# A relational graph layer on one core: the gate's u turned by DMA in two-byte halves instead of by TensorE

## The chip, the cores and the metric

The kernel runs on one core of a Trainium2 chip. The metric is the device time of one execution in microseconds (us). A core has TensorE (PE; its weight loads are listed as PEld), VectorE (DVE), ScalarE (ACT), GpSimd (POOL) and SyncE (SP), each with a queue of its own that it works off in order, and 16 DMA engines that move data for the queues of SP, ACT and POOL. Engines wait for one another by semaphores.

## The reference

With h = relu(layernorm(x)) for 1250 nodes of 1024 values, and 20000 edges of 8 types:

```python
def _rgcn(x, edge_index, edge_type, weight, root, bias):
    ...
    out = x @ root + bias
    for r in range(weight.shape[0]):
        ...
        mean = sums / jnp.maximum(cnt, 1.0)[:, None]
        out = out + mean @ weight[r]
    return out
u = _rgcn(x, edge_index, edge_type, weight, root, bias)
z = jnp.concatenate([u, x], axis=1) @ w_gate + b_gate
h = jnp.tanh(u) * z + x * (1.0 - z)
```

`x` stands here for the layer's input h; what is returned is the first x plus this result. All arrays are float32. The part that matters below is the gate's product u @ w_gate[:1024], which needs u with its columns on the partitions, that is, transposed.

## The kernel before

The nodes lie in 10 blocks of 128 rows (the last has 98), taken in 5 pairs. Each of the matrices (8 weights, root, the two halves of w_gate) is multiplied with a pair of blocks by one call of `product`, which forms seven products of half-size blocks in place of eight. `transposed` puts a block, turned, into the operand tile `h_op` at A11 and A12 (first block of a pair) or A21 and A22 (second block): eight transposes on TensorE into two PSUM banks, then one copy on ScalarE (L378) and one on VectorE (L376). `left` then makes four sums of these on VectorE (L387): S1 = A21 + A22, S2 = S1 - A11, S4 = A12 - S2, S3 = A11 - A21. The seven products of a pair read A11, S1, S2, S4, S3, A12 and A22, in this order (in the last pair A11, A12, S1, S2, S3, S4, A22).

Between the products the results are put together. ScalarE copies the bank after A11 (L457), after S1 (L469), after S2 (L489) and after S3 (L430); VectorE adds after S4 (L423), S3 (L431) and A12 (L448). The products of A11, S2, S3 and A22 go one after the other onto the same bank, those of S1 and S4 onto another, so a product that adds onto a bank starts only after the copy of what stood there.

After each product `product` calls `between(j)`, j from 0 to 6. In the gate, the last of the stages, that is `beside_u` (`beside_last` for pair 5), which issues the work for later pairs. The queues are written out by hand: every engine works in the order in which the program issues. In the gate loop, with i from 0 to 4 for pairs 1 to 5, it is:

- j = 0: gathers of the rows of x + h for pair i (`xhs`), gathers that add z's rows onto the bias that lies in z's place (for pair 1 at j = 3), loads of u for pair i + 2 (L1691, SP) and gathers of its rows of h @ root;
- j = 1: scatters of the finished rows of the pair before (L746);
- j = 2: the bias loads for pair i + 1 (L1649, SP); z * d and + xhs (L1667, L1668, for pair 1 at j = 5); u of pair i + 2 gets its rows of h @ root added (L1611); gathers of h rows for pair i + 1 and its tanh (L1676);
- j = 3: transposes and `left` for pair i + 1;
- j = 4: d = tanh(u) - h for pair i + 1 (L1684);
- j = 3 to 5 and after the last product: `finish` (L1733, L1734), row = product * d + z.

All gathers go by L740 on GpSimd's queue. Those of xhs, of h @ root and of h land in tiles from `got()`, a pool of five buffers of 128 x 1024 float32, given out in program order: a new tile waits until one of the five has been read for the last time. u has a pool of four such buffers.

Of the kernel before, what the change touches and what calls it, by code (L numbers as in the profile page):

```python
# [9 lines left out]
F32 = mybir.dt.float32  # L10
BF16 = mybir.dt.bfloat16
I32 = mybir.dt.int32
AF = mybir.ActivationFunctionType
OP = mybir.AluOpType
AX = mybir.AxisListType
# [4 lines left out]
def tile_rgcn_highway(  # L20
# [31 lines left out]
    nc = tc.nc  # L52
# [3 lines left out]
    P = 128  # L56
# [8 lines left out]
    NP = ND // 2  # L65
# [18 lines left out]
    A11, A12, A22, S1, S2, S3, S4 = range(7)  # L84
    A21 = S3
# [100 lines left out]
    class Second:  # L186
# [22 lines left out]
        def left(self):  # L209
            nc.vector.tensor_add(self.s1, self.a21, self.a22)  # L210
            nc.vector.tensor_sub(self.s2, self.s1, self.a11)
# [152 lines left out]
    def transposed(aop, part, of, n, relu=False):  # L364


        for half, to in enumerate(((A11, A12), (A21, A22))[part]):
            p = bank().rearrange("p (k f) -> p k f", k=KQ)
            for i in range(KQ):
                k = KQ * half + i  # L370
                nc.tensor.transpose(p[:, i, :n], of[:n, k * P:(k + 1) * P], ident[:n, :n])  # L371
            to_n, p_n = aop[:, to, :, :n], p[:, :, :n]
            if half and relu:
                nc.vector.tensor_scalar_max(to_n, p_n, 0.0)
            elif half:
                nc.vector.tensor_copy(to_n, p_n)  # L376
            else:
                nc.scalar.activation(to_n, p_n, AF.Relu if relu else AF.Copy)  # L378
            if n < P:
                nc.gpsimd.memset(aop[:, to, :, n:], 0.0)  # L380

# [354 lines left out]
    h_op = [keep.tile([P, 7, KQ, P], F32, name=f"h_op{i}") for i in range(NP)]  # L736
# [73 lines left out]
    with ExitStack() as early:  # L810
# [483 lines left out]
        while going[0]:  # L1294
            s, i = next(steps)
# [11 lines left out]
    with ExitStack() as edges_part:  # L1307
# [7 lines left out]
        def got():  # L1315
            t = gpool.tile([P, D], F32, name="got")
            if fresh[0]:
                nc.gpsimd.memset(t, 0.0)
                fresh[0] -= 1
            return t  # L1320
# [25 lines left out]
        us = {}  # L1346
# [202 lines left out]
        while s < R0[1]:  # L1549
            step(s, i, on)  # L1550
            s, i = next(steps)
# [14 lines left out]
        s, i = beside(first_group, sum(K[0]) + LATE + 1, s, i, R0[2] - 1)  # L1566
# [46 lines left out]
        def place_of(what, i, part):  # L1613

            o = ("z", "d").index(what)
            if i % 2:
                w = fac[NM - 1].spare[o].rearrange("p k n -> p (k n)")
                return w[:, part * D:(part + 1) * D]
            return h_op[2 + o][:, 2 * part:2 * part + 2].rearrange("p a k f -> p (a k f)")

        def pair(i):
            return [(part, 2 * i + part, nrows(2 * i + part)) for part in range(2)]
# [46 lines left out]

        def gate_u(i, j):  # L1670

            if j == 2:
                for part, d, n in pair(i):
                    hs[part] = got()
                    rows_of(hs[part][:n], h_dram[:, :], node[:n, LG, d:d + 1])
                    nc.scalar.activation(place_of("d", i, part)[:n], us[d][:n], AF.Tanh)  # L1676
            elif j == 3:
                for part, d, n in pair(i):
                    transposed(h_op[i % 2], part, us.pop(d), n)
                left(h_op[i % 2])  # L1680
            elif j == 4:
                for part, d, n in pair(i):
                    dt = place_of("d", i, part)
                    nc.vector.tensor_sub(dt[:n], dt[:n], hs[part][:n])  # L1684

        def gate_load(i, j):

            if j == 0:
                for part, d, n in pair(i):
                    u = new_u(d)  # L1690
                    nc.sync.dma_start(u[:n], last_dram[d * P:d * P + n, :])  # L1691
                    adds.append(add_hr(d, u))
            elif j == 2:
                while adds:
                    adds.pop(0)()
# [28 lines left out]
        for i in range(NP):  # L1724
            t = [rows.tile([P, D], F32, name="row") for _ in range(2)]

            def finish(part, of, c0, more=None):
                d = 2 * i + part
                n = nrows(d)
                at = slice(c0, c0 + of.shape[-1])  # L1730
                to = t[part][:n, at]
                if more is None:
                    nc.vector.tensor_mul(to, of[:n], place_of("d", i, part)[:n, at])  # L1733
                    nc.vector.tensor_add(to, to, place_of("z", i, part)[:n, at])  # L1734
                else:
                    nc.vector.tensor_mul(more[:n], of[:n], place_of("d", i, part)[:n, at])
                    nc.vector.tensor_add(to, to, more[:n])

            def beside_u(j):
                if i == 0 and j == 0:  # L1740
                    fac[NM - 1].make_t4()
                gate_rows(i, j)
                if j == 1:
                    scatter_outs()
                if i + 2 < NP:
                    gate_load(i + 2, j)
                if j == (3 if i else 5):
                    finish(0, t[0][:, Q:], Q)
                if j == (4 if i else 5):
                    finish(1, t[1][:, Q:], Q)  # L1750
                if j == 5:
                    finish(0, t[0][:, :Q], 0)
                    outs.append((2 * i, t[0]))
                if i + 1 < NP:
                    gate_u(i + 1, j)

            def beside_last(j):
                gate_rows(i, j)
                if j == 1:
                    scatter_outs()  # L1760
                elif j == 3:
                    finish(0, t[0][:, :Q], 0)
                    finish(0, t[0][:, Q:], Q)
                elif j == 4:
                    finish(1, t[1][:, Q:], Q)
                    scatter_piece(Q, t[1])
                elif j == 5:
                    outs.append((2 * i, t[0]))
                    scatter_outs()

            def finish_last(of, c0, more=None):
# [37 lines left out]
```

## Time and profile before

| | us |
|---|---|
| median of 20 runs | 1388.38 |
| lowest, highest | 1380.16, 1399.45 |
| profiled execution | 1384.65 |
| its span | 1382.9 |
| TensorE busy | 1338.9 (97%) |
| VectorE busy | 956.0 (69%) |
| GpSimd busy | 572.7 (41%) |
| ScalarE busy | 372.5 (27%) |

The span goes from the first to the last instruction of the profiled execution; 1.75 us lie around it. The gate takes it from 1246.8 on. In the page and the answers of the trace a group is named by line, engine, operation and "out<-in" tiles; the idle time of an engine before it follows in brackets, with what ended it. A matmul of 128 x 512 float32 shows as two instructions, so the four of one product are eight.

### The profile page before, as it was taken

The page shows a single profiled execution, that of the slowest core. Times are in us where ns is not written, and L with a number is a line of the kernel's source. Part 1 is how long each engine was busy: PE and PEld are TensorE (multiplying, and loading weights), DVE is VectorE, ACT ScalarE, POOL GpSimd, SP SyncE. Part 2 cuts the span into 40 slices and gives each one's busy share as a digit, 9 for nine tenths or more (in the row PEclk, how much of TensorE's full clock was granted, in tenths as well). Part 3 has the DMA queues.
Part 4 walks back from the last instruction along what each step waited for, and adds up shares of the span by engine and source line. Part 5 has one row for each costly group of instructions (what it writes and reads, how often), then busy time and mean ns, then how long its engine had stood idle before and what let it go on. Part 6 is the DMA issues. An engine that isn't in the chain of part 4 may idle for free.

```text
span 1382.9 us, 13410 instructions
## 1 busy us (share of the span) xinstructions
PE 1338.9 (97%) x4168; PEld 728.9 (53%) x4168; DVE 956.0 (69%) x1823; ACT 372.5 (27%) x794; POOL 572.7 (41%) x509
## 2 busy tenths in 40 slices
PE   9999979996989999999999999999999999999997
PEld 5444445454535554665565565556556556544443
DVE  7744644573457446745888798788688789867975
ACT  3334535553554121221111112121112111221210
POOL 0000452555155604740345345554545556615631
PEclk9999999998999999999999999999999999999999
DMA  8745334854274424113555777977968976888971
GB/s 320 274 176 166 103 92 101 186 117 97 77 192 98 92 92 106 47 64 139 179 195 201 277 239 277 347 264 247 330 214 290 322 289 199 281 307 249 341 191 57
DMA packets 104319, 270.94 MB, mean 196 GB/s; under 512 B 20100, under 2 KB 22354, under 8 KB 104112
## 3 DMA queue, kind: packets, MB, share of 16 engines
q1 hardware_dynamic: 44048, 119.85, 27.4%
q0 software_dynamic: 44064, 118.20, 26.7%
q10 hardware_dynamic: 16128, 31.98, 7.6%
q8 instruction: 33, 0.54, 0.2%
q14 instruction: 46, 0.38, 0.1%
HBM read 212.63 MB, written 75.49 MB: 208 GB/s over the span
## 4 chain that ended last, share of the span: by engine, by line
PE 84%; issue 4%; DVE 2%; another core or an unknown queue 2%; ACT 1%; POOL 1%; DMA 0%; POOLq 0%; DVEq 0%; ACTq 0%
PE ps_b L406 41%; PE ps L406 15%; PE ps L219 14%; PE ps_n L406 4%; PE ps_b L219 4%; PE ps_q L219 2%; PE ps_q L406 2%; PE ps_n L219 1%; DMA h_op<-in_L_gnn_b_gate_dram 0%; POOL out_dram L746 0%; PE ps L371 0%; DVE junk L1145 0%; ACT is_lo L1055 0%; PE ps_q L1124 0%
## 5 line engine op out<-in xcount | busy, mean ns | idle before, releaser
L406 PE MATMUL ps_b<-w,h_op 128*128 128x512 f32 x1464 | 665.4, 599 | 6.8 <-issue 5.8
L406 PEld LDWEIGHTS ps_b<-w,h_op 128*128 128x128 f32 x1464 | 276.2, 192 | 318.5 <-issue 308.6
L1339 POOL DMA_INDIRECT got<-y,idx x193 | 249.7, 1294 | 287.5 <-DVE u L1344 182.4
L1344 DVE SCALAR_TENSOR_TENSOR u<-got,w_of,u 128x1024 f32<-128x1024 f32 (+1 forms) x193 | 246.9, 1282 | 33.9 <-DMA got<-y,idx 31.5
L406 PE MATMUL ps<-w,h_op 128*128 128x512 f32 (+1 forms) x592 | 266.3, 591 | 0.1
L1163 POOL DMA_INDIRECT table<-row_col,at_i x157 | 167.3, 1066 | 230.2 <-DVE at_i L1159 140.4
L406 PEld LDWEIGHTS ps<-w,h_op 128*128 128x128 f32 x592 | 111.3, 190 | 119.6 <-issue 115.9
L219 PE MATMUL ps<-w,w 128*128 128x256 f32 x288 | 75.3, 396 | 14.3 <-ACT w L225 12.8
L430 ACT COPY row<-ps_b 128x512 f32<-128x512 f32 x53 | 31.1, 586 | 206.5 <-PE ps_b L406 181.8
L431 DVE TENSOR_TENSOR row<-row 128x512 f32<-128x512 f32 x44 | 30.3, 690 | 78.4 <-ACT row L430 78.2
L406 PE MATMUL ps_n<-w,h_op 128*128 128x512 f32 x176 | 80.1, 592 | 0.0
L489 ACT COPY row<-ps_b 128x512 f32<-128x512 f32 x54 | 31.7, 586 | 169.9 <-PE ps_b L406 158.9
L219 PEld LDWEIGHTS ps<-w,w 128*128 128x128 f32 x288 | 56.4, 198 | 38.3 <-issue 15.2
L219 PE MATMUL ps<-w,h_op 128*128 128x256 f32 x288 | 74.5, 381 | 0.0
L1132 DVE TENSOR_TENSOR own<-ps_q,is_at 128x160 f32<-128x160 f32 (+1 forms) x40 | 12.7, 318 | 83.6 <-PE ps_q L1069 31.2
L219 PE MATMUL ps<-inner,inner 128*128 128x256 f32 x264 | 68.6, 383 | 0.0
L219 PEld LDWEIGHTS ps<-w,h_op 128*128 128x128 f32 x288 | 54.0, 190 | 27.1 <-issue 21.9
L529 ACT COPY row<-ps_b 128x512 f32<-128x512 f32 x40 | 23.4, 585 | 162.9 <-PE ps_b L406 130.7
L219 PEld LDWEIGHTS ps<-inner,inner 128*128 128x128 f32 x264 | 50.8, 192 | 14.8 <-issue 8.4
L1145 DVE SCALAR_TENSOR_TENSOR junk<-k_bc,key_col,before 128x128 f32<-128x128 int32 x157 | 55.0, 350 | 4.2
L406 PEld LDWEIGHTS ps_n<-w,h_op 128*128 128x128 f32 x176 | 33.4, 190 | 39.5 <-issue 39.0
L457 ACT COPY row<-ps_b 128x512 f32<-128x512 f32 x54 | 31.7, 587 | 76.2 <-PE ps_b L406 71.3
(238 smaller groups left out, 1508.7 us busy)
## 6 DMA issues: line engine op xcount, KB each, us to landing
y<-row SPq DMA_DIRECT2D x72, 512.0 KB
w<-in_L_gnn_weight_dram ACTq DMA_DIRECT2D x21, 1024.0 KB
w<-in_L_gnn_weight_dram SPq DMA_DIRECT2D x10, 1024.0 KB
k_bc<-keys_dram SPq DMA_DIRECT2D x39, 256.0 KB
l_bc<-los_dram SPq DMA_DIRECT2D x39, 256.0 KB
w<-in_L_gnn_w_gate_dram ACTq DMA_DIRECT2D x6, 1024.0 KB
h_dram<-h_op SPq DMA_DIRECT2D x9, 512.0 KB
u<-in_L_gnn_bias_dram SPq DMA_DIRECT2D x9, 512.0 KB
```

What stands on the lines that cost most here:

```text
L219: nc.tensor.matmul(p, a[:, k, :], b[:, k, :], start=(fresh and k == 0), stop=(k == 1), skip_group_check=True)
L406: nc.tensor.matmul(b[:, at], aop[:, i, k, :], w.of[i][:, k, at], start=(fresh and k == 0), stop=(k == KQ - 1), skip_group_check=True)
L430: nc.scalar.copy(d, b)
L431: nc.vector.tensor_add(c22, c if lone else c22, d)
L457: nc.scalar.copy(c11, b)
L489: nc.scalar.copy(c12, b)
L529: nc.scalar.copy(c21, b)
L1132: nc.vector.tensor_tensor(own[:, :m], looked[:, :m], o["is_at"][:, :m, None, :].to_broadcast([P, m, 2, NHI]), op=OP.mult)
L1145: nc.vector.scalar_tensor_tensor(junk, o["k_bc"][:, i, :], key_col[:, c:c + 1], before, op0=OP.is_equal, op1=OP.mult, accum_out=rank[:, c: ...
L1163: ins = nc.gpsimd.indirect_dma_start(out=table[:, :], out_offset=bass.IndirectOffsetOnAxis(ap=at_i[:n, c:c + 1], axis=0), in_=row_col[:n, ...
L1339: nc.gpsimd.indirect_dma_start(out=t[:n], out_offset=None, in_=y[g][:, :], in_offset=bass.IndirectOffsetOnAxis(ap=at[:n, d, k:k + 1], axis=0),
L1344: nc.vector.scalar_tensor_tensor(u[:n], t[:n], w, u[:n], op0=OP.mult, op1=OP.add)
```

## The change

For pairs 2 to 5 `transposed` is no longer called in the gate. In its place, for each block:

- `in_halves`, at j = 0 for the first and j = 1 for the second block, after its tanh: ScalarE reads u as 2048 two-byte values and writes the first two-byte half of every float32 to the first 1024 places, the second halves behind them, into a tile from `got()`. For the block of 98 rows GpSimd first clears partitions 96 to 127 of it.
- `turned`: SP issues a DMA that transposes, of 128 x 2048 two-byte values, back onto u's own tile.
- `whole_again`, at j = 4: two copies on ScalarE for each block, which put the two halves of each value side by side again in `h_op`.

`left` for these pairs moves from j = 3 to j = 5, and tanh from j = 2 to j = 0 and 1. `gate_u` is called before `finish` and not behind it. Pair 1 is turned by TensorE as before.

```diff
+    def in_halves(of, n, to):
+
+        if n < P:
+            nc.gpsimd.memset(to[n // 32 * 32:], 0.0)
+        nc.scalar.copy(to.bitcast(U16)[:n].rearrange("p (h c) -> p h c", h=2),
+                       of.bitcast(U16)[:n].rearrange("p (c h) -> p h c", h=2))
+
+    def turned(of, to):
+
+        nc.sync.dma_start_transpose(to.bitcast(U16).rearrange("p (c r) -> p c r", r=P),
+                                    of.bitcast(U16))
+
+    def whole_again(aop, part, of, n):
+
+        of = of.bitcast(U16).rearrange("p (h a k r) -> p h a k r", h=2, a=2, r=P)
+        for a, to in enumerate(((A11, A12), (A21, A22))[part]):
+            nc.scalar.copy(aop[:, to].bitcast(U16).rearrange("p k (r h) -> p h k r", h=2)[..., :n],
+                           of[:, :, a, :, :n])
             if n < P:
                 nc.gpsimd.memset(aop[:, to, :, n:], 0.0)
...
         def gate_u(i, j):
 
-            if j == 2:
+            if j < 2 and i:
+                part, d, n = pair(i)[j]
+                nc.scalar.activation(place_of("d", i, part)[:n], us[d][:n], AF.Tanh)
+                halves = got()
+                in_halves(us[d], n, halves)
+                turned(halves, us[d])
+            elif j == 2:
                 for part, d, n in pair(i):
                     hs[part] = got()
                     rows_of(hs[part][:n], h_dram[:, :], node[:n, LG, d:d + 1])
-                    nc.scalar.activation(place_of("d", i, part)[:n], us[d][:n], AF.Tanh)
-            elif j == 3:
+                    if not i:
+                        nc.scalar.activation(place_of("d", i, part)[:n], us[d][:n], AF.Tanh)
+            elif j == 3 and not i:
                 for part, d, n in pair(i):
                     transposed(h_op[i % 2], part, us.pop(d), n)
                 left(h_op[i % 2])
             elif j == 4:
                 for part, d, n in pair(i):
+                    if i:
+                        whole_again(h_op[i % 2], part, us.pop(d), n)
                     dt = place_of("d", i, part)
                     nc.vector.tensor_sub(dt[:n], dt[:n], hs[part][:n])
+            elif j == 5 and i:
+                left(h_op[i % 2])
...
                 if i + 2 < NP:
                     gate_load(i + 2, j)
+                if i + 1 < NP:
+                    gate_u(i + 1, j)
                 if j == (3 if i else 5):
                     finish(0, t[0][:, Q:], Q)
...
-                if i + 1 < NP:
-                    gate_u(i + 1, j)
```

More of the change, by code (lines that the diff above doesn't have):

```diff
@@ L12 @@
 I32 = mybir.dt.int32
+U16 = mybir.dt.uint16
 AF = mybir.ActivationFunctionType
@@ L378, in transposed @@
                 nc.scalar.activation(to_n, p_n, AF.Relu if relu else AF.Copy)
+            if n < P:
+                nc.gpsimd.memset(aop[:, to, :, n:], 0.0)
+    def in_halves(of, n, to):
+        if n < P:
+            nc.gpsimd.memset(to[n // 32 * 32:], 0.0)
[9 more added lines that the diff above has]
+                           of[:, :, a, :, :n])
             if n < P:
```

## The prediction

> I number the pairs 1 to 5 and name a pair's seven products by their left operands, in the order in which TensorE runs them: A11, S1, S2, S4, S3, A12, A22 (in pair 5: A11, A12, S1, S2, S3, S4, A22). All stamps are us from the start of the span.
>
> **What bounds the kernel now.** I read the page first: TensorE is busy for 97% of the span, at nine tenths or more of its clock in every slice, so what matters is what leaves its queue and what makes it wait:
>
> ```profile
> PE 1338.9 (97%) x4168; PEld 728.9 (53%) x4168; DVE 956.0 (69%) x1823; ACT 372.5 (27%) x794; POOL 572.7 (41%) x509
> ```
>
> Then the chain of waits in the gate (start, length, what):
>
> ```profile
> 1283.07 3.43 PE ps_n L406 x8
> 1286.51 1.75 PE ps L371 x16
> 1288.25 3.44 PE ps_b L406 x8
> ...
> 1326.31 6.24 DMA h_op<-in_L_gnn_b_gate_dram
> ```
>
> A product takes 3.43, the transposes of a pair 1.75 between two products, and nothing waits. The last line is the one landing of a 512 KB load that the chain shows: 6.2 us with gathers beside it. Third, the timelines of ScalarE, VectorE and GpSimd around pair 1, beside which pair 2 is turned (start, busy, engine, line, operation; in brackets the idle time before it and what ended that):
>
> ```profile
> 1250.46 0.59 ACT L457 COPY row<-ps_b 128x512 f32<-128x512 f32 x1 [6.28 <-PE ps_b L406]
> 1253.89 0.59 ACT L469 COPY row<-ps_n 128x512 f32<-128x512 f32 x1 [2.85 <-PE ps_n L406]
> 1257.33 0.59 ACT L489 COPY row<-ps_b 128x512 f32<-128x512 f32 x1 [2.85 <-PE ps_b L406]
> 1257.81 2.01 ACT L1676 ACTIVATE w<-u 128x1024 f32<-128x1024 f32 x2
> ...
> 1258.17 2.49 DVE L1611 TENSOR_TENSOR u<-u,got 128x1024 f32<-128x1024 f32 x2 [6.12 <-DMA u<-last_dram]
> 1263.30 2.75 DVE L387 TENSOR_TENSOR h_op<-h_op 128x512 f32<-128x512 f32 x4
> 1271.53 1.23 DVE L1667 TENSOR_TENSOR h_op<-h_op,h_op 128x1024 f32<-128x1024 f32 x1 [1.41 <-DMA h_op<-z_dram,node]
> ...
> 1259.67 1.81 POOL L740 DMA_INDIRECT got<-h_dram,node  x1 [9.59 <-DMA w<-in_L_gnn_b_gate_dram]
> 1261.78 1.56 POOL L740 DMA_INDIRECT h_op<-z_dram,node  x1 [0.30 <-PE ps L371]
> ```
>
> To be seen: ScalarE is idle between its copies, but each copy must be out before TensorE adds onto the same bank two products later (L489 before S3). VectorE waits for pair 3's u until 1258.17 and for pair 1's z until 1271.53. GpSimd's gather of h rows at 1259.67 started when the first L1611 ended (1258.17 + 1.25 = 1259.4), not at the DMA that the profile names: it lacked a `got` buffer. The five buffers are the scarce thing. Last, busy time in the stretches of pairs 1 and 2 (PE, PEld, DVE, ACT, POOL; then clock, share of the DMA engines, GB/s):
>
> ```profile
> 1246.80:1272.60 25.80, 25.80 (x73) 12.34 (x72) 17.09 (x18) 5.45 (x8) 12.62 (x9) 1.00 0.86 259
> 1272.60:1298.40 25.80, 25.80 (x74) 12.35 (x73) 25.21 (x32) 5.44 (x8) 16.08 (x14) 1.00 1.02 335
> ```
>
> ScalarE works 5.4 of 25.8 us; the DMA engines are full beside pair 2 (1.02).
>
> **Removed.** 64 transposes. By the starts of the products around them (1260.56 to 1262.31, 1286.34 to 1288.09, 1312.13 to 1313.87, and 1.55 for the last pair, 1337.91 to 1339.46) they hold TensorE 1.75 + 1.75 + 1.75 + 1.55 = 6.8 us. That is the most the change can gain by itself. Eight L378 copies of 0.60 leave ScalarE and eight L376 of 0.68 VectorE, neither on the path.
>
> **Added on ScalarE.** 512 values take 0.59 and 1024 take 1.05 (half of 2.01), so 2048 two-byte values take about 1.05 + 2 x 0.46 = 2.0, and each of the four copies back, 1024 values, 1.05. No row shows a two-byte copy with a stride. Bounds: half (two values a step) and twice. I take 2.0 and 1.05, as the rows of 512 values in bf16 elsewhere (0.63) are near those in f32. Per pair 8.2 us are added and 1.2 leave: 12.4 of 24. In time, from the start of a pair's A11: copy out at 4.2, tanh 5.3, first parting 7.3, second copy 7.9, tanh 8.95, second parting 10.95, L489 11.55, and S3 needs it at 13.7. Covered by 2.1 us, if nothing waits. The copies back follow S3's copy (at 4.2 after S3's start) and end at 8.4; the next A11 needs the first of them by 10.3, S1 needs the last and one `left` (0.7) by 13.7. Covered by some 4.5 us.
>
> **Added waits.** The turn is a new kind of transfer, of 512 KB, on SP's queue. Nearest row: 6.24 to land, from which 4 (an empty engine) to 12 (twice the row) bound it; I take 6.2. Part by part:
>
> *A buffer for the second half.* At j = 1 two buffers hold xh, two hr and one the first half. So the second parting waits until the first turn has landed, or L1611 or L1668 frees another. L489 stands behind it on ScalarE, and S3 behind that.
> Pair 1: first parting ends 1254.1; its turn lands 1254.1 + 6.2 = 1260.3. L1611 frees a buffer at 1259.4: parting to 1261.5, L489 to 1262.1, S3 at 1262.2. Before it was 1262.31: the 1.75 are lost to 0.1.
> Pair 2: its A11 starts at 1272.5 (three products after 1262.2), so its first parting ends at 1279.8; the delay found below puts its S1 at 1280.2 and S3 at 1290.5. With 2.7 for parting, L489 and the step to TensorE, a landing of up to 8.0 us is covered: 0.
> Pair 3: turn issued at 7.3, landed 13.5, parted 15.5, L489 16.1, S3 at 16.2 in place of 13.7: +2.5; if L1668's buffer is handed out, which VectorE frees after some 10 us, 0. I take the middle, +1.25.
> Pair 4: nothing is loaded for a sixth pair, so two buffers are free: 0.
>
> *`left` behind the gate's rows.* `left` moves from j = 3 to j = 5, and beside pair 1 the z rows are multiplied at j = 5, ahead of it on VectorE. The h gathers now find a buffer at 1260.4 (first turn) and 1260.7 (second L1611); at 2.1 us each the z gathers follow at 1264.6, not 1261.78, 2.8 later. z was waited for until 1271.53, so now 1271.5 (pair 3's u loads, which shared the DMA engines, come later) to 1274.4. Two L1667 and two L1668 take 4.9, `left`'s S1 another 0.8: ready at 1277.2 to 1280.1, 0.1 before TensorE has it. Pair 2's S1 started at 1276.04: +1.2 to +4.2. I take +4.2, because GpSimd's order is certain and the relief is not.
>
> *Queues passed.* SP: the turns stand ahead of the bias loads, and the u loads wait for the copies back; biases are used a pair later, u 13 us later. GpSimd gets one more memset, at the last pair (0.23 in its nearest row). VectorE's added wait is `left`; `finish` stands behind it, and no product waits for that within 20 us.
>
> A rule is weighed here against the row of 6.24. The Trainium skill, "VectorE: DVE Perf Modes", section "The three transpose paths", gives 1309 ns for a 128x128 two-byte block by DMA and 390 ns on TensorE; 16 blocks one after the other would be an estimated 21 us a turn, and the change some 20 us slower. Its page "DMA: Bandwidth & Descriptors", section "Latency and other measured facts", gives 261 GB/s instead, an estimated 2 us for 512 KB plus the start. No row here decides between them.
>
> **Sum.** Pair 1: +4.2 (at pair 2's S1, its own 1.75 used up in it). Pair 2: -1.75. Pair 3: -1.75 + 1.25. Pair 4: -1.55. Together +0.4 us. The profiled execution took 1384.65 (span 1382.9 and 1.75 around it), 3.7 below the median of 1388.38; the same difference goes on both. Forecast 1388.8: no change that can be told, for which 0.3% (4.2 us) is the bound. Its own range: +1.2 at pair 1 and no wait, -3.9; waits of 2 and 2.5 at pairs 2 and 3 on top of +4.2, +3.7: 1384.5 to 1392.1.
>
> **Rivals.**
> *Late turns (slower).* Beside pairs 2 and 3 the DMA engines are at 1.02 and 0.90, and a turn has to share them. At 12 us: pair 1's turn lands at 1266.1, the second h gather takes its buffer then, z is 3.6 later, +7.8. Pair 2 -1.75 and about 1 of waits; pair 3 -1.75 and about 3 at S3; pair 4 -1.55 and 1 at S1: some +7.8, 1396. It decides from a landing of about 9 us: past 6.5 each us costs one at z and about half of one at S3 and S1.
> *z in time (faster).* If z lands by 1269, `left` is ready by 1274.7, ahead of pair 2's S1 at 1275.9. Then -0.1 - 1.75 - 1.75 - 1.55 = -5.2: 1383.2. For it speaks that u loads no longer run beside z, against it the later issue.
> *Slow parting.* At twice the time per value, from A11's start: 3.65 + 3 x 0.6 + 2 x 1.05 + 2 x 4 = 15.5 for L489 against 13.7: 1.8 lost in each pair, as much as is saved, and pair 1's +4.2 stays: 1392.5.
> *Not done.* If transposes stayed on TensorE, L371 would still show 80 for u: no reason for that in the diff.
>
> **How the numbers follow.** Forecast 0.50 (of it 0.41 within 0.3%, 0.07 slower, 0.02 faster), late turns 0.28 (all slower), slow parting 0.10 (0.08 slower), z in time 0.12 (0.10 faster). Faster 0.12, same 0.45, slower 0.43. The range runs from z in time with a little more, 1382.5, to late turns of some 17 us, 1402.
>
> **What would show it.** L371 has 16 for u in place of 80. The turns' landing is 6 us; L489 beside pairs 1 and 3 waits behind a parting, and S3 with it; L387 for pair 2 starts after L1668, and pair 2's S1 waits for it 1 to 4 us; beside pair 4 nothing waits. Wrong, if the turns land in 4 us or in 12, if a parting takes 1 us or 4, or if z comes by 1269.

## The result and the profile after

The changed kernel takes 1413.41 us (median of 9 runs, 1406.84 to 1417.83) where the kernel before took 1388.47: ratio 1.018, 95% interval 1.016 to 1.020. It is slower by some 25 us; the forecast was 1388.8, range 1382.5 to 1402.0. The profiled execution of the changed kernel took 1416.32 us, its span is 1414.5. The text calls one DMA that transposes a block a turn, and the copy of `in_halves` ahead of it a parting. Line numbers behind L386 are 22 higher than before, in the gate's own code up to 33: L428 is the product (L406), L409 `left` (L387), L491 and L511 the copies after S1 and S2 (L469, L489), L762 the gathers (L740), L1715 the subtraction d = tanh(u) - h (L1684), L1689 z * d (L1667).

First the page's line of engines. TensorE has 64 transposes less, and its share is smaller, not larger; the groups say what its idle time ended with (busy, mean ns, then idle and releaser).

```profile
PE 1340.9 (95%) x4104; PEld 725.4 (51%) x4104; DVE 951.5 (67%) x1815; ACT 401.8 (28%) x810; POOL 574.1 (41%) x510
...
L428 PE MATMUL ps_n<-w,h_op 128*128 128x512 f32 x176 | 86.4, 631 | 20.7 <-DVE h_op L409 20.7
```

TensorE's timeline in the gate has four waits that were not there before, at S3 of pair 1 and at S1 of pairs 2, 3 and 4 (start, busy, engine, line; in brackets the idle time before it and what ended it):

```profile
1269.20 3.70 PE L428 MATMUL ps_b<-w,h_op 128*128 128x512 f32 x8 [0.42 <-ACT row L511]
...
1290.25 6.35 PE L428 MATMUL ps_n<-w,h_op 128*128 128x512 f32 x8 [7.04 <-DVE h_op L409]
...
1323.22 5.23 PE L428 MATMUL ps_n<-w,h_op 128*128 128x512 f32 x8 [6.02 <-DVE h_op L409]
...
1356.72 5.55 PE L428 MATMUL ps_n<-w,h_op 128*128 128x512 f32 x8 [7.66 <-DVE h_op L409]
```

Two things cost time here. S1 waits for `left`, and then it takes 5.2 to 6.4 in place of 3.6, because the granted clock has dropped: the stretches of these three products, with their columns PE, PEld, DVE, ACT, POOL, then clock, share of the DMA engines, GB/s, are

```profile
1290.25:1296.45 6.20, 6.20 (x9) 2.62 (x10) 6.06 (x10) 0.91 (x1) 3.03 (x4) 0.57 1.06 263
1323.22:1328.30 5.08, 5.08 (x9) 2.28 (x10) 4.98 (x8) 2.45 (x2) 1.27 (x3) 0.69 1.04 269
1356.72:1362.10 5.38, 5.38 (x8) 2.36 (x9) 5.20 (x8) 2.75 (x2) 3.56 (x6) 0.65 0.87 149
```

The clock was 1.00 through the same products before. From the start of a pair's A11 to the next the books balance to 0.3, with a product at 3.43 from start to start:

| | before | after | worked out from the rows |
|---|---|---|---|
| pair 1 | 25.78 | 24.71 | -1.75 transposes, +0.42 at S3 |
| pair 2 | 25.78 | 34.00 | -1.75, +7.04 wait, +2.76 slow S1 (6.19 to the next start) |
| pair 3 | 25.78 | 31.85 | -1.75, +6.02, +1.64 (5.07) |
| pair 4 | 25.62 | 33.82 | -1.55, +7.66, +1.95 (5.38) |
| pair 5 and the end | 33.1 | 35.2 | its z rows came late |

Together +23.5 in the gate; the medians differ by 24.9. (The rest of the difference between the two profiled executions, 8 us, lies before the gate, in code that the change does not touch.)

Why is `left` late? VectorE's timeline shows what stands ahead of it: the subtraction, which waits for rows of h, beside pair 1 the z rows too.

```profile
1280.01 1.22 DVE L1715 TENSOR_TENSOR w<-w,got 128x1024 f32<-128x1024 f32 x1 [4.21 <-DMA got<-h_dram,node]
...
1283.38 1.22 DVE L1689 TENSOR_TENSOR h_op<-h_op,h_op 128x1024 f32<-128x1024 f32 x1 [1.55 <-DMA h_op<-z_dram,node]
...
1316.07 1.23 DVE L1715 TENSOR_TENSOR h_op<-h_op,got 128x1024 f32<-128x1024 f32 x1 [7.83 <-DMA got<-h_dram,node]
1319.41 1.23 DVE L1715 TENSOR_TENSOR h_op<-h_op,got 128x1024 f32<-128x1024 f32 x1 [2.12 <-DMA got<-h_dram,node]
...
1322.48 2.74 DVE L409 TENSOR_TENSOR h_op<-h_op 128x512 f32<-128x512 f32 x4
```

GpSimd's timeline shows why the rows of h are late, and ScalarE's when the turns landed (L399 are the copies back, L387 a parting). The first line is a gather of z rows for pair 1:

```profile
1270.79 1.56 POOL L762 DMA_INDIRECT h_op<-z_dram,node  x1 [0.30 <-issue]
...
1308.65 0.97 POOL L762 DMA_INDIRECT got<-h_dram,node  x1 [9.10 <-DMA u<-got]
...
1355.34 1.56 POOL L762 DMA_INDIRECT w<-z_dram,node  x1 [12.39 <-DMA w<-in_L_gnn_b_gate_dram]
```

```profile
1340.08 2.53 ACT L399 COPY h_op<-u 128x1024 uint16<-128x1024 uint16 x2 [0.70 <-DMA u<-got]
1352.65 2.52 ACT L399 COPY h_op<-u 128x1024 uint16<-128x1024 uint16 x2 [10.05 <-DMA u<-got]
...
1360.32 1.89 ACT L387 COPY got<-u 128x2048 uint16<-128x2048 uint16 x1
```

The h gather at 1308.65 waited 9.10 for a `got` buffer that a turn still held. The turns of pair 4 were issued at 1328.73 and 1332.79 and landed at 1340.0 and 1352.6: 11.3 and 19.8 us. At pair 4 the copies back thus ended at 1355.17, 0.8 before `left` began, so there the late turn would have held S1 almost as long by itself. The queues' packets in the gate (packets, MB, share of the 16 engines' time), before and after over the window 1246 to 1383 us:

```profile
q0 software_dynamic: 5872, 20.88, 52.6%
q1 hardware_dynamic: 2208, 8.02, 16.4%
```

```profile
q0 software_dynamic: 4962, 17.90, 49.3%
q1 hardware_dynamic: 18649, 11.52, 47.0%
```

SP's queue has 16441 packets more, nearly all of them the turns' 256-byte ones (a turn by itself shows 2080), and its share is larger by 30.6% of 137 us of all 16 engines, 42 us or some 5 us a turn. The engines, busy for 69% of that window before, are now busy for 96%.

### The profile page after: what moved, and what is told of

Its sections match the earlier page's. It is cut to its first block, busy times and chain, and to the rows that moved or that the text cites. A ratio compares the mean times of both kernels' runs of the same rounds, so it can differ in the third digit from the quotient of the medians.

```text
span 1414.5 us, 13321 instructions
## 1 busy us (share of the span) xinstructions
PE 1340.9 (95%) x4104; PEld 725.4 (51%) x4104; DVE 951.5 (67%) x1815; ACT 401.8 (28%) x810; POOL 574.1 (41%) x510
## 4 chain that ended last, share of the span: by engine, by line
PE 80%; DMA 5%; issue 4%; DVE 3%; another core or an unknown queue 1%; ACT 1%; POOL 1%; SPq 0%; POOLq 0%; DVEq 0%; ACTq 0%
PE ps_b L428 38%; PE ps L428 15%; PE ps L220 14%; PE ps_b L220 4%; PE ps_n L428 4%; PE ps_q L220 2%; DMA got<-h_dram,node 2%; PE ps_n L220 1%; PE ps_q L428 1%; DMA h_op<-z_dram,node 1%; DMA h_op<-in_L_gnn_b_gate_dram 1%; DMA u<-got 1%; DVE h_op L409 1%; DMA u<-last_dram 0%
## 5 line engine op out<-in xcount | busy, mean ns | idle before, releaser
L428 PE MATMUL ps_b<-w,h_op 128*128 128x512 f32 x1464 | 667.8, 601 | 11.5 <-issue 10.1
L428 PEld LDWEIGHTS ps_b<-w,h_op 128*128 128x128 f32 x1464 | 277.3, 192 | 326.6 <-issue 313.7
L428 PE MATMUL ps<-w,h_op 128*128 128x512 f32 (+1 forms) x592 | 264.8, 589 | 0.1
L428 PEld LDWEIGHTS ps<-w,h_op 128*128 128x128 f32 x592 | 111.0, 190 | 119.2 <-issue 115.1
L428 PE MATMUL ps_n<-w,h_op 128*128 128x512 f32 x176 | 86.4, 631 | 20.7 <-DVE h_op L409 20.7
L452 ACT COPY row<-ps_b 128x512 f32<-128x512 f32 x53 | 31.1, 586 | 209.9 <-PE ps_b L428 202.3
L511 ACT COPY row<-ps_b 128x512 f32<-128x512 f32 x54 | 31.6, 586 | 167.0 <-PE ps_b L428 151.7
L551 ACT COPY row<-ps_b 128x512 f32<-128x512 f32 x40 | 23.4, 585 | 168.4 <-PE ps_b L428 128.0
L428 PEld LDWEIGHTS ps_n<-w,h_op 128*128 128x128 f32 x176 | 35.6, 204 | 65.0 <-issue 41.2
L1077 ACT ACTIVATE is_lo<-io,less_lo 128x128 bf16<-128x128 f32 x157 | 50.2, 393 | 0.7 <-DMA xh_dram<-xt 0.7
```

Of the source, the lines that this page charges most:

```text
L428: nc.tensor.matmul(b[:, at], aop[:, i, k, :], w.of[i][:, k, at], start=(fresh and k == 0), stop=(k == KQ - 1), skip_group_check=True)
L452: nc.scalar.copy(d, b)
L511: nc.scalar.copy(c12, b)
L551: nc.scalar.copy(c21, b)
L1077: nc.scalar.activation(is_lo[:, i, :], io, AF.Abs, bias=less_lo[:, c0 + i:c0 + i + 1])
```

## The experiments

Each ratio is to runs of the kernel before in the same session, because the level of both moved between sessions (before took 1388, 1337 and 1383 us). The changed kernel itself was measured at the level of 1388 only; where a ratio of the later sessions is set against its 1.018, it is taken that this carries over.

My theories after the result: **A**, the five buffers (turns hold them, gathers of h wait, `left` waits behind the subtraction); **B**, traffic (turns and gathers slow each other down); **C**, the order on VectorE (what stands ahead of `left`); **D**, the clock after TensorE's idling. The rival to all four is the new order by itself.

### The order without the turns

```diff
                 nc.scalar.activation(place_of("d", i, part)[:n], us[d][:n], AF.Tanh)
-                halves = got()
-                in_halves(us[d], n, halves)
-                turned(halves, us[d])
...
-                        whole_again(h_op[i % 2], part, us.pop(d), n)
+                        transposed(h_op[i % 2], part, us.pop(d), n)
```

> The order of the changed kernel with TensorE's transposes in it: gate_u ahead of finish, tanh at j = 0 and 1, transposes at j = 4, left at j = 5; no parting, no turn, no copies back, no buffers taken. If the turns are the cause of the 25 us (all my theories but one), it is within 4 us of the kernel before: 1386 to 1392, with at most 1 to 2 us of wait at S1 of pair 2. If the new order by itself is the cause (rival), S1 of pairs 2 to 4 waits several us each and it is 1400 or more.

Ratio 1.0013 (0.9992 to 1.0035), and no wait at any S1. The order alone costs nothing that can be told. `left` stood behind the z rows beside pair 1 here as well, and was in time.

### Own buffers, and `left` first

```diff
-                halves = got()
+                halves = h_op[4][:, 2 * part:2 * part + 2].rearrange("p a k f -> p (a k f)")
```

> The changed kernel with the halves in h_op[4], which is idle in the gate, so that the turns take none of the five buffers; all else as in the changed kernel. Theory A (buffers: h gathers wait for buffers that the turns hold, sub and so left wait for the h gathers): S1 of pairs 2 to 4 waits 2 us or less each in place of 6.0 to 7.7, TensorE's clock stays up, about 1390 to 1394. Theory B (traffic: the turns and the gathers slow each other down wherever they meet): turns still land in 10 us and more, S1 of two of the pairs still waits 4 us or more, 1400 to 1408.

Ratio 1.0183 (1.0139 to 1.0228): nothing won. TensorE's and SP's timelines, where pair 4 is turned beside pair 3:

```profile
1352.68 6.37 PE L428 MATMUL ps_b<-w,h_op 128*128 128x512 f32 x8 [13.21 <-ACT h_op L399]
```

```profile
1322.23 26.84 SPq L392 DMA_TRANSPOSE u<-h_op  x2
```

The gathers no longer waited for a buffer, so all four of h and xh went out between 1325 and 1331, together with the two turns. The turns were back 29 us after the first was issued (copies back at 1351.30), and A11 of pair 4 waited 13.21. Theory A is wrong in a useful way: at this pair the wait for a buffer had kept gathers and turns apart.

```diff
-            elif j == 5 and i:
-                left(h_op[i % 2])
...
+                if i:
+                    left(h_op[i % 2])
                 for part, d, n in pair(i):
                     dt = place_of("d", i, part)
                     nc.vector.tensor_sub(dt[:n], dt[:n], hs[part][:n])
```

> The changed kernel with left right behind the copies back, ahead of the subtraction d = tanh(u) - h and of the z rows on VectorE. Theory C (order on VectorE: what stands ahead of left holds it up, not the turns): from the copies back of the changed kernel's trace (ended 1283.04, 1312.92, 1355.17) S1 of pair 2 waits 0.5, of pair 3 nothing, of pair 4 still 5 to 6, some 17 us less than 7.0 + 6.0 and their slow products: 1396 to 1400. Theory B: the turns are late enough by themselves, S1 still waits 4 us or more in all three pairs: 1405 or more.

Ratio 1.0180 (1.0146 to 1.0214). C gave the right places and the wrong sum. S1 of pairs 3 and 4 no longer waits; S1 of pair 2 still waits 5.29 (its second turn was back at 1281.6). But new waits stand at S4:

```profile
1301.24 6.17 PE L428 MATMUL ps_n<-w,h_op 128*128 128x512 f32 x8 [7.09 <-ACT row L491]
...
1331.84 6.24 PE L428 MATMUL ps_n<-w,h_op 128*128 128x512 f32 x8 [3.82 <-ACT row L491]
```

```profile
1297.86 1.06 ACT L1696 ACTIVATE h_op<-u 128x1024 f32<-128x1024 f32 x1 [13.30 <-DVE row L1767]
```

ScalarE's copy after S1 (L491), which S4 needs, now stands behind the tanh of j = 0; that waits until `finish` of the pair before has read d's place, and `finish` waits on VectorE behind the subtraction and the z rows, whose rows are still late.

> Both edits, own buffers for the halves and left right behind the copies back. A and C together: no wait at S1 over 1 us, the transposes' 6.8 us are won: 1382 to 1388. Theory B: the second turn of a pair lands 15 to 20 us after its issue where gathers run beside it, S1 of pair 4 at least waits 3 us or more with a half-clock product behind it: 1392 to 1400.

Both edits together: 1.0279 (1.0247 to 1.0311), slower than either, and slower than either theory had it. `left` waits for the copies back, and what stands behind `left` on VectorE waits with it: the second turn of pair 5 came 21 us after its issue, and A12 of pair 5 waited 15.44 for an addition behind `left`. Neither edit takes the loss away.

### The turn left out, and a plain copy in its place

```diff
-                turned(halves, us[d])
...
-        of = of.bitcast(U16).rearrange("p (h a k r) -> p h a k r", h=2, a=2, r=P)
+        of = of.bitcast(U16).rearrange("p (a k r h) -> p h a k r", h=2, a=2, r=P)
...
```

(GpSimd also clears the rows of u that the last block of 98 leaves empty.)

> The changed kernel without the DMA that transposes: parting, five buffers, copies back (which read u as it was loaded, so the gate's product gets u unturned) and the new order stay. Theory B (the turns' traffic is the whole loss): S1 of pairs 2 to 4 waits for nothing or up to 3 us at pair 2, where the z rows stand ahead of left, 1380 to 1387. Rival (ScalarE: 8.2 us more a pair and a tanh that waits for finish hold up the copies that TensorE needs): waits of 1 us and more for ScalarE in every pair, 1393 or more.

Ratio 0.9955 (0.9939 to 0.9972): 6.0 us faster (3.7 to 8.2). One wait of the change remains in the gate:

```profile
1235.95 3.70 PE L428 MATMUL ps_n<-w,h_op 128*128 128x512 f32 x8 [1.54 <-ACT row L491]
```

That is S4 of pair 2, behind a tanh that waited for `finish`; 6.8 of transposes less 1.5 is 5.3, inside the interval. So parting, copies back, queue order and `left` at j = 5 cost some 1.5 us in all, and the DMA costs the rest.

```diff
-        nc.sync.dma_start_transpose(to.bitcast(U16).rearrange("p (c r) -> p c r", r=P),
-                                    of.bitcast(U16))
+        nc.sync.dma_start(to.bitcast(U16), of.bitcast(U16))
```

> The changed kernel with a plain copy of the same 512 KB from the same buffer to u in place of the DMA that transposes (the gate's product gets u unturned); queue, order, waits and bytes stay. If the transposing form is what costs (many small packets): the copies land in 4 to 7 us and it is 1381 to 1392. If 512 KB more on full DMA engines cost this in any form: S1 waits 4 us and more again, 1403 or more.

Ratio 1.0024 (1.0014 to 1.0034), 9 us above no transfer and 21 below the turns (1.018 - 1.0024, of 1337). The same bytes in plain packets cost one wait, at S1 of pair 2:

```profile
1235.95 5.94 PE L427 MATMUL ps_n<-w,h_op 128*128 128x512 f32 x8 [7.20 <-DVE h_op L408]
```

-6.8 + 7.2 + 2.3 for the slow product (5.94 less 3.60) is +2.7; the ratio makes it 3.2. So the bytes alone undo the gain, beside pair 1, where the z rows now land later; the transposing form costs 21 us more. Beside the other pairs the plain copies cost no wait, although the DMA engines' share was 1.04 beside pair 3 (1258.4 to 1282.4, 352 GB/s). Whether it is the 256-byte packets or the transposing itself that makes the difference, no run tells apart.

### Transfers by themselves

```diff
+    def turn(k):
+        nc.sync.dma_start_transpose(u[k].bitcast(U16).rearrange("p (c r) -> p c r", r=P),
+                                    halves[k].bitcast(U16))
+    def plain(k):
+        nc.sync.dma_start(u[k], halves[k])
+    def gather(k):
+        nc.gpsimd.indirect_dma_start(
+            out=got[k], out_offset=None, in_=x[:, :],
+            in_offset=bass.IndirectOffsetOnAxis(ap=at, axis=0))
```

> No layer is computed: the kernel runs 14 groups of transfers twice each, every group started only when the one before has landed, and copies x to the output. Groups, of 512 KB transfers: one turn (T), one plain copy from SBUF to SBUF (C), one load (L), one broadcast bias load (B), one gather of 128 rows (G); two turns, two copies, two gathers, four gathers; two turns, two copies or two loads with four gathers; two turns or two copies with two bias loads behind them. Theory B1 (a turn is quick alone and slow only in company: its packets and the gathers' hold each other up): T lands in 3 to 4 us, two turns with four gathers take over 1.3 times the sum of two turns and four gathers run apart. Theory B2 (the transfers only add up, and the DMA engines were full): TTGGGG takes at most that sum. A turn that is slow by itself: T takes 6 us or more, T over twice C.

> No layer is computed: groups of transfers as in the first kernel of this kind, each started when the one before has landed. Two turns on SP's queue (TT) alone, with one, two and four gathers beside them, with four loads, four stores or two plain copies from ScalarE's queue beside them; four half-size turns with four gathers; one turn on SP's and one on ScalarE's queue, alone and with four gathers; and the loads, stores and copies alone. Theory G (it takes a gather's packets, of the software queue): with loads or copies of the same bytes beside it the second turn is seen within 1.2 times the sum of the two run apart, with gathers it is later than that. Theory P (any 4 KB packets slow the turns' 256-byte packets): four loads delay the second turn as much as four gathers do, to 15 us or more. With one gather the delay is under 5 us, with two between, with four 12 us, in both.

VectorE reads each target as soon as it has landed, so its timeline gives the landings. Two turns alone were released at 61.37, two turns with four gathers at 127.92, two plain copies with four gathers at 169.67:

```profile
65.75 0.17 DVE L78 COPY junk<-u 128x8 uint16<-128x8 uint16 x1 [4.38 <-DMA u<-halves]
68.16 0.17 DVE L78 COPY junk<-u 128x8 uint16<-128x8 uint16 x1 [2.25 <-DMA u<-halves]
...
134.51 0.17 DVE L78 COPY junk<-u 128x8 uint16<-128x8 uint16 x1 [6.59 <-DMA u<-halves]
146.82 0.17 DVE L78 COPY junk<-u 128x8 uint16<-128x8 uint16 x1 [12.14 <-DMA u<-halves]
...
172.56 0.17 DVE L78 COPY junk<-u 128x8 uint16<-128x8 uint16 x1 [2.89 <-DMA u<-halves]
174.96 0.17 DVE L78 COPY junk<-u 128x8 uint16<-128x8 uint16 x1 [2.23 <-DMA u<-halves]
```

| from release until the last one of the group is seen, us | first time, second time |
|---|---|
| one turn | 4.4, 4.3 |
| two turns (first kernel; second kernel) | 6.8, 6.7; 6.6, 6.5 |
| two plain copies | 4.2, 4.2 |
| four gathers | 10.3, 9.9 |
| two turns with one, two gathers | 9.1, 9.0; 10.8, 10.8 |
| two turns with four gathers (first; second) | 18.9, 19.4; 15.3, 17.8 |
| two plain copies with four gathers | 10.4; 13.2 with two more loads |
| four loads; with two turns | 8.0, 8.3; 11.5, 12.8 |
| four stores; with two turns | 6.4, 4.9 (begun early); 12.5, 12.4 |
| two copies from ScalarE's queue with two turns | 9.1, 8.9 |
| four half-size turns with four gathers | 17.6, 15.4 |
| one turn from SP's queue, then one from ScalarE's, issued when the first had landed | 8.5, 8.3 |
| the same with four gathers | 12.6, 14.3 |
| two turns with two bias loads behind them | 10.9, 10.7 |

(Loads into u waited for u only. So in the second round of the two plain copies with four gathers the next group's two loads went along, 2.10 MB on SP's queue in place of 1.05, and the groups of loads with gathers can't be read. The second round of stores began before the first had ended.)

No theory of these two kernels is right as I put it. A turn alone is quick, 4.4 us and 2.4 for one behind it. Two plain copies hide under four gathers (10.4 against 10.1). Two turns do not: with gathers they take 15.3 to 19.4, about the sum of the two run one after the other (6.7 + 10.1 = 16.8), and it is the second turn that is late. Loads and stores do it to a smaller degree (12 against 6.6), so it does not take a gather; with gathers it is worst. Two turns one strictly after the other lost less (12.6 and 14.3 with four gathers) than two on one queue, though alone they took longer (8.4 against 6.6). What happens inside is to be seen in the queues' shares, for a turn alone (window 11.2 to 15.6) and for the tail of the group with four gathers (143 to 146.5):

```profile
q1 hardware_dynamic: 2080, 0.52, 63.0%
```

```profile
q1 hardware_dynamic: 755, 0.19, 99.4%
q0 software_dynamic: 48, 0.17, 12.1%
```

63.0% of 4.4 us of 16 engines are 44 us for 2080 packets, 21 ns for one of 256 bytes; 99.4% of 3.5 us are 56 us for 755, 74 ns each, although the gathers hold only 12% of the engines' time there.

The plainest rival is that the engines' time simply adds up; the shares of the whole groups answer it. Alone, two turns took 5.6 us of all 16 engines (81.5% of 6.9), two plain copies 2.6 (61.0% of 4.3), four gathers 6.3 (61.8% of 10.2). Copies and gathers together took 8.7 (81.8% of 10.6), no more than the 8.9 of the two apart, and they fit into the time that the gathers leave. Turns and gathers together took 18.9 (99.1% of 19.1, the group from 127.92 on) where apart they take 11.9. So a turn holds the engines twice as long as a plain copy of the same bytes, which alone keeps two of them from hiding, and in company the packets become slower on top of that.

### Kept busy

```diff
                 c = inner.hold() if inner and inner.holds else held("ps_n")
+                for _ in range(warm):
+                    add(c, A11, True)
                 add(c, S1, True)
```

(`warm` is 2 in pairs 2 to 4; pair 5, which the expectation names too, has none.)

> The changed kernel with the product of A11 run twice more by TensorE into S1's bank ahead of S1 in pairs 2 to 5 (overwritten by S1's own start), so that TensorE works 6.9 us through its wait. Theory D (the slow S1 comes from the clock that is granted after 6 to 8 us of idling): S1 takes 3.4 to 3.7 in pairs 2 to 4 in place of 6.35, 5.23 and 5.55, which is worth 6 us; pair 5, which does not wait there, pays about 0 to 3: 1407 to 1412. If the slow S1 has another cause: it still takes 5 and more, 1414 to 1420.

Ratio 1.0150 (1.0120 to 1.0180), with six products more than needed, 20.6 us of TensorE's work, in what had been waits. S1 of pairs 2 and 4:

```profile
1234.99 3.70 PE L428 MATMUL ps_n<-w,h_op 128*128 128x512 f32 x8 [0.37 <-DVE h_op L409]
...
1299.63 3.70 PE L428 MATMUL ps_n<-w,h_op 128*128 128x512 f32 x8 [0.48 <-DVE h_op L409]
```

D holds: with TensorE at work until then S1 takes 3.70, while in the same session 7.20 of idling made it 5.94 (the plain copy's line above). The whole does not differ from the changed kernel by more than the intervals.

### Less of it

```diff
-                halves = got()
-                in_halves(us[d], n, halves)
-                turned(halves, us[d])
+                if not part:
+                    halves = got()
+                    in_halves(us[d], n, halves)
+                    turned(halves, us[d])
...
-                        whole_again(h_op[i % 2], part, us.pop(d), n)
+                        (transposed if part else whole_again)(h_op[i % 2], part, us.pop(d), n)
```

> The changed kernel with only the first block of each pair turned by DMA; the second is transposed by TensorE at j = 4. Half of the removed work comes back (3.4 us), half of the added traffic goes, and no turn stands behind another. If the loss is in proportion to the turns' bytes, half of it stays: ratio 1.009. If it is the meeting of two turns with the gathers (the second turn of a pair and the gathers that it holds up): S1 of pairs 2 to 4 waits 2 us or less, ratio 0.999 to 1.005.

Ratio 1.0052 (1.0036 to 1.0067): half the turns keep under a third of the loss, so it is not in proportion; but it is a little above the second case too. S1 of pairs 2 to 4 waits 3.47, 0.73 and 1.43, and A11 of pair 4 waits 2.27 for a copy back.

```diff
-            if j == 2 and i + 1 < NP:
-                gate_bias(i + 1)
+            if i == 0 and j == 0:
+                nc.sync.dma_start(bias_rows, b_gate[None, :].to_broadcast([P, D]))
+            if j == 5 and i + 1 < NP:
+                for part, d, n in pair(i + 1):
+                    nc.scalar.copy(place_of("z", i + 1, part)[:n], bias_rows[:n])
```

> The changed kernel with b_gate loaded once into h_op[4] and copied by ScalarE to z's places at j = 5, in place of eight 512 KB loads that stand behind the turns on SP's queue. The z gathers then wait for no bias (12 us beside pairs 4 and 5 in the changed kernel) and 4 MB less meet the turns. Traffic theory: S1 waits 2 to 5 us in place of 6.0 to 7.7 and the last pair's z is in time, ratio 1.006 to 1.013. If only turns and the gathers of h decide: waits as they were, ratio 1.016 or more.

Ratio 1.0126 (1.0104 to 1.0148), a third of the loss gone, as traffic would have it. But the edit does two things: it takes 4 MB off the engines, and it frees the z gathers from biases that stand behind the turns on SP's queue. Which of the two won the third is not shown.

```diff
-            if j < 2 and i:
+            last = i == NP - 1
+            if j < 2 and last:
...
-            elif j == 3 and not i:
+            elif j == 3 and not last:
...
-            elif j == 5 and i:
+            elif j == 5 and last:
```

> The change for pair 5 alone, which is turned beside pair 4, where neither u nor h @ root is loaded for a later pair; pairs 2 to 4 are transposed by TensorE, all in the order of the kernel before. At most 1.55 us can be won. Traffic theory: with two h gathers, two xh gathers and two biases beside them the turns land in 7 to 14 us; the last z rows come later, by 0 to 3 us: ratio 0.999 to 1.003. If one pair carries a quarter of the loss wherever it lies: 1.0045 or more.

Ratio 0.9991 (0.9982 to 1.0000). Pair 5 alone carries none of the loss: its turns were issued at 1284.46 and 1288.5, ScalarE waited 2.26 for the first, its four copies ran through from 1297.68 on, and no product waited.

### Without company, and pair 5 once more

```diff
                     hs[part] = got()
-                    rows_of(hs[part][:n], h_dram[:, :], node[:n, LG, d:d + 1])
+                    if i:
+                        nc.gpsimd.memset(hs[part][:n], 0.0)
+                    else:
+                        rows_of(hs[part][:n], h_dram[:, :], node[:n, LG, d:d + 1])
```

(the same for xh)

> The changed kernel with the sixteen gathers of h and xh rows of pairs 2 to 5 left out (GpSimd clears their tiles instead, so the output lacks these terms); turns, order, buffers, u loads, biases, z and h @ root gathers stay. Theory B (the gathers beside the turns): turns land in 4.5 to 9 us, S1 of pairs 2 to 4 waits 2 us or less each, ratio 0.995 to 1.004. If the turns are late for another reason: they land in 10 us and more, S1 waits 4 us and more, ratio 1.012 or more.

Ratio 0.9990 (0.9959 to 1.0020), with all eight turns in it. They were back before ScalarE came to the copies, but for one wait of 0.82 (the first of pair 4, issued at 1308.80 and waited for until 1320.58, some 11.7 us), and of the waits at S1 one was left, at pair 2 behind the z rows:

```profile
1279.16 5.24 PE L428 MATMUL ps_n<-w,h_op 128*128 128x512 f32 x8 [2.44 <-DVE h_op L409]
```

In the gate itself it thus takes the gathers of h and xh for the loss to arise; with u loads, biases, z gathers and scatters beside them the turns just use up the gain. The edit also spares the subtraction ahead of `left` its wait for rows of h, so how much of the loss is the gathers' own lateness and how much that of the turns is not taken apart.

```diff
-                halves = got()
+                halves = h_op[4][:, 2 * part:2 * part + 2].rearrange("p a k f -> p (a k f)")
...
-            if j == 2 and i + 1 < NP:
+            if j == (0 if i == NP - 2 else 2) and i + 1 < NP:
                 gate_bias(i + 1)
```

(and `left` ahead of the subtraction, on top of the edit for pair 5 alone)

> The change for pair 5 alone (as in the run of that kind before, ratio 0.9991), its halves in h_op[4] so that the xh gather, which waited 11.4 us for a turned buffer, waits for none; its two biases loaded at j = 0 ahead of the turns; left ahead of the subtraction. Most that can be won is 1.55 us, 0.12%: ratio 0.9985 to 0.9995 if the z rows of pair 5 come earlier; 1.000 or more if gathers that now run beside the turns make these late.

Ratio 1.0116 (1.0069 to 1.0164): a miss by 16 us for two turns, with A11 of pair 5 the one that waits.

```profile
1362.88 5.45 PE L428 MATMUL ps_b<-w,h_op 128*128 128x512 f32 x8 [15.75 <-ACT h_op L399]
```

```profile
1329.92 32.15 SPq L392 DMA_TRANSPOSE u<-h_op  x2
```

With buffers of their own for the halves and the biases early, nothing held GpSimd back: two h, two xh and two z gathers went out from 1328.43 to 1337.5, and the turns came back at 1361.5 and 1366.4, 32 us and 28 us after their issue. Queue shares in the stretch 1344 to 1350:

```profile
q0 software_dynamic: 158, 0.57, 72.7%
q1 hardware_dynamic: 452, 0.12, 40.0%
```

That is 0.69 MB in 6 us, 115 GB/s from engines that show 113% busy: 442 ns for a packet of the gathers and 85 ns for one of the turns. (Four gathers alone took 61.8% of 10.2 us of 16 engines for 576 packets, 175 ns each.) In the run of pair 5 alone further up (ratio 0.9991) the second xh gather waited 11.42 us for a turned buffer, and the turns were back in time. The three edits of this kernel weren't taken apart; that the buffers are what matters is argued from the own-buffer run above, where they were the only edit and the turns took 29 us.

## Why the prediction was wrong

**Right.** The transposes' 6.8 us: without the turn 6.0 were won, against one wait of 1.5. L372, which was L371, has 16 for u. A parting takes 1.89 (2.0 was taken). S3 of pair 1 waited for L511 behind a parting, though 0.42 and not the 1.65 that "lost to 0.1" meant. The place of the main loss, S1 behind a `left` that stands behind the z rows, was named for pair 2. Copies back take 1.26 each, not 1.05, and their cover held that.

**The step that failed: the turn's landing, "I take 6.2".** It was taken from a load with gathers beside it, as if a turn were one more 512 KB load. Alone it is better than that (4.4, and 2.4 more for the second). In the gate it took 11.8 for the second block of pair 2, 9.4 for the first of pair 3, 11.3 and 19.8 for pair 4, 11.8 and 15.3 for pair 5. The bound of 12 was twice the row; nothing in the trace of before shows a transposing transfer, so no row could bound it from above, and I should have said that instead of doubling. The DMA engines' share of 1.02 beside pair 2, already shown, was a warning, but it is no price either: at 1.04 plain copies of the same bytes cost no wait. What the row of a load left out is that a turn holds the engines twice as long as a plain copy (2.8 against 1.3 us of all 16), and that in company both it and the gathers become slower. The Trainium skill's page "DMA: Bandwidth & Descriptors", section "Latency and other measured facts", gives 261 GB/s for a transposing DMA; alone it moved some 215 GB/s here (0.52 MB in 2.4 us); with gathers beside turns the two queues together moved 115 in the stretch shown above.

**"Pair 2: -1.75. Pair 3: -1.75 + 1.25. Pair 4: -1.55."** These were the pairs of which only S3 was priced, and S3 was never late there. The subtraction also stands ahead of `left` (j = 4 before j = 5), it needs the rows of h, and their gather needs a buffer that a turn holds. I had that chain for the z rows beside pair 1 alone. By the prediction the periods of pairs 2, 3 and 4 were to change by +2.45 (the +4.2 in it), -0.5 and -1.55; they grew by 8.2, 6.1 and 8.2.

**Pair 1's +4.2 for `left` behind the z rows** was 0 with the order alone and with the turn left out, 7.2 with a plain copy and 7.04 with the turns. It was mostly the traffic that made the z rows late, not GpSimd's order: counted from A11 of pair 1, their first gather was issued 0.9 later than before (1270.79 after 1254.89, 1261.78 after 1246.83), not the 2.8 of the prediction, and its rows were seen 3.8 later (1283.38, 1271.53).

**"`finish` stands behind it, and no product waits for that within 20 us."** Wrong: the tanh of j = 0 needs d's place from `finish`, and the copy after S1 stands behind it on ScalarE. S4 waits 1.54 for that without the turn, and 7.09 with `left` first.

**Not priced at all:** the clock. Three products after a wait took 6.35 us more together (2.76 + 1.64 + 1.95).

**The rival.** Late turns (1396, chance 0.28) was the right mechanism with the right sign. Its 7.8 for the z rows, at S1 of pair 2, is near the 7.04 measured; too low were the 12 us for a turn at most (19.8 came) and the waits of 1 to 3 us in the pairs behind it, where 6.02 and 7.66 came at S1, and it had no price for the slow products.

**What stays open.** Why 256-byte packets of a turn and 4 KB packets of a gather hold each other up is not settled. The gathers need not fill the engines for it (74 ns a packet at 12% of their time), and plain packets of the same queue do not suffer (copies and gathers together took 8.7 us of the engines, 8.9 apart). Small packets that don't transpose were not tried.

## What to carry to other kernels

Before a transfer of a new kind is added beside others, time that kind in that company: neither the row of a single transfer nor the DMA share of the stretch is a price for it (at 1.04 plain copies cost no wait here, beside pairs 2 and 3 turns of the same bytes cost 6 to 8 us each). Ask how long it holds the engines, and what lands last behind it. A transposing DMA is a matter of company: 2.4 to 4.4 us alone, 9 to 32 beside gathers; if it is used, put it where few gathers run, as for pair 5 here (0.9991), and look at what keeps them apart before you take a wait away; here a lack of buffers seems to have done it. When a wait moves an operand's last step on one engine, list all that stands ahead of that step in program order, and what each of those waits for in turn.

## What the runs showed of the hardware

- A product that follows an idle TensorE runs slower: after 6.0 to 7.7 us of waiting 5.2 to 6.4 in place of 3.6, at a granted clock of 0.57 to 0.69. It also happened after 2.06 (5.40, `left` first) and 2.44 (5.24, less company), but not after 3.90 in the run with both edits (3.70) nor after 1.54 (3.70). The Trainium skill, "TensorE: Matmul & The Clock Gate", section "What's actually happening", has the half rate begin after at least one idle window of about 3.4 us and end after as long at work, with a window that runs on freely. The runs agree that it takes some idling; waits of 2.06 and 2.44 were shorter than that window and had a slow product all the same. With a free window 3.90 without one is no contradiction.
- Two 512 KB turns and four 512 KB gathers take as long together as one after the other (15.3 to 19.4 us against 16.8), where two plain copies of the same size are hidden by the gathers (10.4 against 10.1); with six gathers the two turns took 36 us (1329.92 to 1366.4).
- Engines that show over 100% busy can move as little as 115 GB/s, where plain copies with gathers moved 300 on average over their whole group (3.15 MB in 10.4 us).
